# Values and ones in one tile, division by tokens, and PSUM drained by two engines in two attention layers

## The chip, the cores and the metric

The kernel runs on one core of a Trainium2 chip. Its engines are TensorE (PE in the profile; PEld are its weight loads), VectorE (DVE), ScalarE (ACT), GpSimd (POOL) and SyncE (SP, which issues most DMA transfers). The metric is the time of one execution on the device in microseconds; a version is told by the median of its runs.

## What is computed

The reference is a chain of eight layers, four attentions and four feed-forward layers, each applied to the layer-normed activation and added to it. The input is 8 batches of 512 tokens with 128 features. Only the first and the third layer matter here. Cut to their core:

```python
# first attention: 16 heads of 8
q, k, v = proj(Wq), proj(Wk), proj(Wv)
for start in range(0, S, 128):                 # queries start .. start+127
    scores = q[start:start+128] @ k[:start+128].T / sqrt(8)
    scores = where(triu(ones(128, start+128), k=1), neg, scores)
    out[start:start+128] = softmax(scores) @ v[:start+128]
y = out @ Wo

# second attention: linear, 64 features per head
qf, kf = relu(q @ Wf + bf), relu(k @ Wf + bf)
kv = einsum('blhf,blhd->bhfd', kf, v)
num = einsum('blhf,bhfd->blhd', qf, kv)
den = maximum(einsum('blhf,bhf->blh', qf, kf.sum(axis=1)), 1e-6)
y = (num / den) @ Wo + bo
```

The mask of the first attention hides, for the query with index i inside its window, every key with an index above i counted from the start of the sequence. So only the first 128 keys are ever seen, and one 128 x 128 triangle serves all four windows.

## The kernel before

The activation lives in SBUF as eight tiles `X[b]` of 128 tokens x 4 token blocks x 128 features. The function `l0_l1_ffn` runs the first four layers in one stage (the change is only there); later stages run the other four layers.

In that stage the work of a batch is a chain of generators, and each `yield` ends a piece. `scores` (first attention up to the maxima) and `exps` with `add_up` (exponentials and weighted sums, four head rows `r` per batch) and `give` (division, output projection) are followed by `experts` (the routed feed-forward layer), `features` (second attention) and `router` (router of the fourth layer). A loop at the end of the stage takes one piece of every generator in flight in each step, so that several batches overlap: in a step of even number the next `exps`, in a step of odd number the sums. A new batch starts every eight steps, and `scores` runs 13 steps ahead. After the last batch of the first attention, pieces of the shared experts (`shared`, L369 to L384) are put in between.

This is the program's order. A scheduler of the framework then fixes one order of instructions for each engine, which departs from it in places; each engine works through its own list in order and waits by semaphores where it needs another's result.

Heads are packed four to a 32-partition group. A group is called a quad here: four matmuls of 32 rows or 32 columns, one per quad, run side by side on the array.

- Scores, L533 to L551: for each token block `c`, four matmuls fill two PSUM tiles `halves` of two banks each (tag "two", two such tiles in all). ScalarE copies each half to `sm` (L542), GpSimd masks it (L543), VectorE reduces it to the negated maxima (L547).
- Exponentials, L558 to L581: scores again, keys on the partitions, plus the maxima by a second matmul, into the same two PSUM tiles; ScalarE takes the exponential into `eT` (L575, four buffers), GpSimd masks (L577).
- Sums, L584 to L594: for every row `r` one set of four matmuls with the values `vq` as the stationary operand into `o0`, and one set with `own`, a tile of ones, into `o1`: the latter holds the softmax sums, repeated 8 times over the partitions of a head. `vq` holds the values of head row `r` in the columns of that row and zeros elsewhere (L524).
- Division, L596 to L601: reciprocal of `o1`, 128 x 512, and a product with `o0`, both on VectorE. Then the output projection (L606).
- Second attention, L733 to L834: features of the keys (L762, L767 into "two", relu by ScalarE at L773 into `wide[:, 0]`), of the queries (L783, relu at L788 into `wide[:, 1]`), products `kv` with the values `v` and with a tile of ones `one` (L797), masking by head (L802), transposes (L262 through `flipped`), product with the query features for numerator and denominator (L814), then maximum, reciprocal, copy and product (L819 to L823) on VectorE, ScalarE and GpSimd.

PSUM has eight banks of 128 x 512 float32: four are the two tiles "two", two the tiles "mm" that everything else shares, and two `o0` and `o1`. The tile `wide` later takes the expert table of the fourth layer; its load is issued in the last batch of `features`. In the first ten steps after the leading ones, DMA transfers fill a DRAM buffer with zeros out of a tile `zeros`.

Of the kernel before, what the change touches and what calls it, by code (L numbers as in the profile page):

```python
# [67 lines left out]
def eight_layers(ctx: ExitStack, tc: tile.TileContext, w: dict, out: bass.AP):  # L68
# [171 lines left out]
    def cols(c):  # L240
        return slice(c * P, (c + 1) * P)
# [28 lines left out]
    def l0_l1_ffn():  # L270
# [28 lines left out]
        with ExitStack() as es:  # L299
# [101 lines left out]
            with ExitStack() as es1:  # L401
# [9 lines left out]
                own = keep.tile([P, 4, 4, HD], F32, tag="own", name="own")  # L411
                nc.gpsimd.memset(own, 1.0)
                nc.gpsimd.affine_select(
                    out=own, in_=own, compare_op=ALU.is_equal, fill=0.0, base=0,
                    pattern=[[1, 4], [-1, 4], [0, HD]], channel_multiplier=0,
                )
                own = own.rearrange("p r s d -> p r (s d)")
# [15 lines left out]

                maxima = [keep.tile([P, C, 4, 32], BF16, tag=f"mx{i}", name=f"mx{i}") for i in range(2)]
# [10 lines left out]
                zeros = keep.tile([P, C, 4, 32], F32, tag="zeros", name="zeros")  # L445
# [53 lines left out]
                one = keep.tile([P, 32], F32, tag="one", name="one")  # L499
                nc.vector.memset(one, 1.0)  # L500

                ready = {}

                def scores(b):

                    stats(b, mv0)
                    for got in normal(b, mv0, work):
# [15 lines left out]
                    vq = work.tile([P, 4, 4, 32], F32, tag="vq", name="vq", bufs=3)  # L523
                    nc.vector.tensor_tensor(  # L524
                        vq,
                        mm[:, P : 2 * P].rearrange("p (q f) -> p q f", q=4).unsqueeze(2)
                        .to_broadcast([P, 4, 4, 32]),
                        own.unsqueeze(1).to_broadcast([P, 4, 4, 32]), ALU.mult,
                    )
# [3 lines left out]
                    for c in range(C):  # L533
                        halves = [two("sc").rearrange("p i (r k) -> p (i r) k", k=P) for i in range(2)]
                        for q in range(4):
                            nc.tensor.matmul(  # L536
                                halves[q // 2][:, 4 * (q % 2) : 4 * (q % 2) + 4, :],
                                qT[quad(q), cols(c)], kb[quad(q)], start=True, stop=True,
                            )
                        for i in range(2):  # L540
                            sm = work.tile([P, 8, P], F32, tag="sm", name="sm", bufs=2)
                            nc.scalar.copy(sm, halves[i])  # L542
                            nc.gpsimd.affine_select(  # L543
                                out=sm, in_=sm, compare_op=ALU.is_ge, fill=-1e30, base=0,
                                pattern=[[0, 8], [-1, P]], channel_multiplier=1,
                            )
# [37 lines left out]
                def add_up(b, r, i, eT):  # L584

                    if r == 0:
                        sums_of[b, i] = ps.tile([P, S], F32, tag=f"o{i}", name=f"o{i}", bufs=1)
# [1397 lines left out]
```

## Time and profile before

| | |
|---|---|
| median of 3 runs | 1713.37 us (1712.08 to 1717.24) |
| profiled execution, its own time | 1725.08 us |
| its span from first to last instruction | 1723.3 us |
| PE busy | 1470.0 us, 85% of the span |
| PEld busy | 651.2 us, 38% |
| DVE busy | 1206.9 us, 70% |
| ACT busy | 796.6 us, 46% |
| POOL busy | 677.8 us, 39% |
| mean granted TensorE clock | 0.935 |
| first to last start of a first-attention exponential score matmul (L568) | 40.7 to 428.7 us |
| last start of a second-attention product (L814) | 607.6 us |

Busy times of one execution are added up by engine; matmuls overlap, so a busy PE need not be at its peak. A group of instructions is shown with its line, engine and operation, output and input tile, shapes and count, then busy us and mean ns of one, then the idle time of the engine just before them and whose work ended it. Lines are those of the kernel before.

### The profile page before, as it was taken

How to read it: one execution, taken by the hardware profiler on the slowest of the kernel's cores; microseconds unless marked ns; L12 is line 12 of the kernel's file. 1: busy time of each engine (PE TensorE's matmuls, PEld its weight loads, DVE VectorE, ACT ScalarE, POOL GpSimd, SP SyncE). 2: the span in 40 equal slices, each digit the busy share in tenths (PEclk: the TensorE clock that was granted, in tenths of full speed). 3: DMA queues.
4: the chain of work that ended last, by engine and by line, in shares of the span. 5: the costliest groups of instructions: out<-in, count | busy, mean ns of one | idle time of the engine just before them, and what ended most of it. 6: DMA issues, size and time to landing. Idle time of an engine off the chain costs nothing.

```text
span 1723.3 us, 22463 instructions
## 1 busy us (share of the span) xinstructions
PE 1470.0 (85%) x8060; PEld 651.2 (38%) x8061; DVE 1206.9 (70%) x2374; ACT 796.6 (46%) x1158; POOL 677.8 (39%) x728
## 2 busy tenths in 40 slices
PE   5978898899888868988999896977888888888887
PEld 2322333334344435644555453422222222233335
DVE  7688666655654444357775764589899999988765
ACT  3655655555454423353223230055555565565634
POOL 4754344443321140211213318135645645712750
PEclk8999899999899889988999898999899999999988
DMA  7991000000000022304544653634444444443201
GB/s 270 384 342 34 1 1 13 7 13 13 13 19 19 13 99 78 95 10 109 124 116 118 134 126 95 151 80 129 124 127 128 133 129 125 131 117 95 61 13 31
DMA packets 94224, 164.69 MB, mean 96 GB/s; under 512 B 10848, under 2 KB 36960, under 8 KB 90016
## 3 DMA queue, kind: packets, MB, share of 16 engines
q1 hardware_dynamic: 89392, 151.97, 31.4%
q0 software_dynamic: 3568, 9.18, 1.7%
q10 hardware_dynamic: 1152, 2.10, 0.4%
q8 instruction: 64, 1.05, 0.3%
q14 instruction: 48, 0.39, 0.1%
HBM read 110.27 MB, written 52.95 MB: 95 GB/s over the span
## 4 chain that ended last, share of the span: by engine, by line
PE 43%; DVE 28%; issue 10%; POOL 7%; ACT 5%; DMA 5%; SPq 1%; DVEq 0%; POOLq 0%; ACTq 0%
DVE h L1890 11%; PE key L1644 5%; PE acc L1622 5%; PE bx L1879 3%; DMA gx<-du_d 2%; PE mm L262 2%; PE sT L568 2%; DVE mf L547 2%; PE o L591 2%; PE sc L536 1%; PE gu L369 1%; PE gu L1055 1%; DMA gate<-gates 1%; DVE zx L1698 1%; PE Z L1690 1%
## 5 line engine op out<-in xcount | busy, mean ns | idle before, releaser
L1890 DVE TENSOR_TENSOR_SCAN h<-a,bx 128x1024 f32<-128x1024 f32 x192 | 426.9, 2269 | 29.2 <-PE bx L1879 27.7
L1885 ACT ACTIVATE a<-dr,nA 128x1022 f32<-128x1022 f32 x192 | 219.4, 1146 | 221.2 <-DVE h L1890 221.0
L1879 PE MATMUL bx<-gx,wb 64*128 64x512 f32 x768 | 220.2, 666 | 61.3 <-DVE h L1890 59.2
L1335 POOL TENSOR_TENSOR gx<-gx,xk 128x1024 f32<-128x1024 f32 x32 | 75.4, 2357 | 226.0 <-DMA gx<-du_d 194.3
L1644 PE MATMUL key<-xT,L_ffn_keys 128*128 128x512 f32 x256 | 136.4, 615 | 22.9 <-DVE act L1648 22.9
L1879 PEld LDWEIGHTS bx<-gx,wb 64*128 64x128 f32 x768 | 64.8, 195 | 195.1 <-DVE h L1890 149.8
L1622 PE MATMUL acc<-act,L_ffn_values 128*128 128x512 f32 x256 | 132.7, 602 | 0.0
L1648 DVE SCALAR_TENSOR_TENSOR act<-key,gate 128x512 f32<-128x512 f32 x128 | 86.5, 685 | 47.8 <-PE key L1644 34.6
L1690 PE MATMUL Z<-h,wc 64*32 64x512 f32 x1536 | 110.3, 628 | 0.1
L547 DVE TENSOR_REDUCE mf<-sm 128x8 f32<-128x1024 f32 x64 | 76.1, 1211 | 42.5 <-POOL sm L543 42.4
L577 POOL TENSOR_SCALAR_AFFINE_SELECT eT<-eT 128x1024 f32<-128x1024 f32 x64 | 68.9, 1099 | 78.7 <-ACT eT L575 78.7
L543 POOL TENSOR_SCALAR_AFFINE_SELECT sm<-sm 128x1024 f32<-128x1024 f32 x64 | 69.4, 1098 | 71.2 <-ACT sm L542 70.9
L1433 POOL DMA_INDIRECT back<-f_out,back_at x32 | 30.8, 964 | 155.7 <-DVE bn L248 139.3
L542 ACT COPY sm<-sc 128x1024 f32<-128x1024 f32 x64 | 62.5, 1014 | 54.7 <-PE sc L536 40.6
L1410 ACT COPY oT<-acc 128x512 f32<-128x512 f32 x8 | 4.7, 587 | 159.2 <-PE acc L1622 159.2
L575 ACT ACTIVATE eT<-sT 128x1024 f32<-128x1024 f32 x64 | 62.0, 1021 | 28.0 <-PE sT L568 27.9
L1644 PEld LDWEIGHTS key<-xT,L_ffn_keys 128*128 128x128 f32 x256 | 47.1, 195 | 73.2 <-issue 36.2
L1622 PEld LDWEIGHTS acc<-act,L_ffn_values 128*128 128x128 f32 x256 | 49.1, 193 | 60.0 <-issue 60.0
L536 PE MATMUL sc<-kb,qT 32*128 32x512 f32 x256 | 58.9, 724 | 10.0 <-ACT sm L542 4.1
L248 DVE BATCH_NORM_STATS2 bn<-x 128x6 f32<-128x128 f32 x224 | 56.1, 272 | 4.8 <-DMA x<-in_L_attn_hidden_states 4.0
L1116 POOL TENSOR_TENSOR rstd<-rstd,minus_half 128x4 f32<-128x4 f32 x27 | 28.0, 1040 | 80.0 <-DVE rstd L1115 79.8
L568 PE MATMUL sT<-qT,kb 32*128 32x512 f32 x256 | 55.2, 655 | 4.5 <-ACT sm L542 2.9
(482 smaller groups left out, 3006.4 us busy)
## 6 DMA issues: line engine op xcount, KB each, us to landing
f_in<-zeros SPq DMA_DIRECT2D x10, 3584.0 KB
gate<-gates SPq DMA_DIRECT2D x128, 256.0 KB
dr<-dt_d SPq DMA_DIRECT2D x32, 1024.0 KB
gx<-du_d SPq DMA_DIRECT2D x128, 128.0 KB
xk<-xh_d SPq DMA_DIRECT2D x32, 256.0 KB
wide<-in_L_ffn_experts SPq DMA_DIRECT2D x1, 3072.0 KB
xg<-f_in SPq DMA_DIRECT2D x48, 64.0 KB
f_out<-ys SPq DMA_DIRECT2D x12, 256.0 KB
```

The costliest lines, as they stand in the source:

```text
L536: nc.tensor.matmul(halves[q // 2][:, 4 * (q % 2) : 4 * (q % 2) + 4, :], qT[quad(q), cols(c)], kb[quad(q)], start=True, stop=True,)
L543: nc.gpsimd.affine_select(out=sm, in_=sm, compare_op=ALU.is_ge, fill=-1e30, base=0, pattern=[[0, 8], [-1, P]], channel_multiplier=1,)
L547: nc.vector.tensor_reduce(mf[:, c, 2 * i : 2 * i + 2], sm.rearrange("p (q r) k -> p q r k", q=2), AX.X, ALU.max, negate=True,)
L568: nc.tensor.matmul(halves[q // 2][:, q % 2, :], lhs[quad(q), r, :], rhs[quad(q)], start=(k == 0), stop=(k == 1),)
L1335: nc.gpsimd.tensor_tensor(gx, gx, xk.unsqueeze(1).to_broadcast([P, 2, S]), ALU.mult)
L1622: nc.tensor.matmul(acc, f2_v[:, j, :], act, start=(j == 0), stop=(j == J - 1))
L1644: nc.tensor.matmul(key, f2_k[:, 2 * j : 2 * j + 2, :], xT, start=True, stop=True)
L1648: nc.vector.scalar_tensor_tensor(act, key, 0.0, gate[:, j % 2, :], ALU.max, ALU.mult)
L1690: nc.tensor.matmul(zs[q][32 * j : 32 * j + 32, i, :], wcf[half, g, :], hs[j // 2][half, j % 2, :], start=(g == 0), stop=(g == G - 1),)
L1879: nc.tensor.matmul(bx[:, k, :], wbf[half, g, :], gx[half, j, :], start=True, stop=True,)
L1885: nc.scalar.activation(a[:, :, 1:], dr[:, 2 * j : 2 * j + 2, 1:], AF.Exp, scale=nA[:, q, g : g + 1],)
L1890: nc.vector.tensor_tensor_scan(h.rearrange("p r t -> p (r t)"), a.rearrange("p r t -> p (r t)"), bx.rearrange("p r t -> p (r t)"), 0.0, AL ...
```

## The change

For the first attention, the values and a block of ones now share one stationary tile: of its 32 columns, for two heads 8 columns of values and 8 of ones each. Three such tiles are kept and their zeros and ones are written once by GpSimd; per batch VectorE copies in only the values (four copies). One set of matmuls per row gives values and sums together; rows 0 and 1 go to `o0`, rows 2 and 3 to `o1`. For the second attention the tile `vo` does the same, with `kv`, its mask (`m2` in place of `m4`), its transposes and the final product in half the matmuls.

The division is a new generator, `divided`, used by both attentions: ScalarE copies the two PSUM tiles to `both`; TensorE transposes them, so that tokens are on the partitions and a head's sum is one number; VectorE takes reciprocals of 32 numbers per token block set and multiplies; the result `a` is transposed back (`flipped`, with ScalarE's copy to `aT`).

In the scores, the second half is masked by a bfloat16 matmul that adds `later_keys` (0 or -1e30) through the identity, and VectorE reduces it straight out of PSUM; the first half goes the old way. The relus of the second halves of key and query features move from ScalarE to VectorE. `eT` has two buffers in place of four, `zeros` is a part of `wide`, and `own` and `one` are gone.

```diff
+                def divided(tiles, least):
+                    both = work.tile([P, 2, S], F32, tag="both", name="both", bufs=2)
+                    for i in range(2):
+                        nc.scalar.copy(both[:, i], tiles[i])
+                    yield True
+                    a = work.tile([P, C, D], F32, tag="toks", name="toks", bufs=2)
+                    for i in range(2):
+                        mm = mm_four()
+                        for c in range(C):
+                            nc.tensor.transpose(mm[:, c, :], both[:, i, cols(c)], ident)
+                        mm = mm.rearrange("p c (n k d) -> p (c n) k d", k=2, d=HD)
+                        rd = work.tile([P, 8 * C, 1], F32, tag="rd", name="rd", bufs=2)
+                        if least is None:
+                            nc.vector.reciprocal(rd, mm[:, :, 1, 0:1])
+                        else:
+                            nc.vector.tensor_scalar(rd, mm[:, :, 1, 0:1], least, None, ALU.max)
+                            nc.vector.reciprocal(rd, rd)
+                        nc.vector.tensor_tensor(
...
+                    yield True
+                    aT = work.tile([P, S], F32, tag="aT", name="aT", bufs=2)
+                    flipped(a, mm_four(), aT)
+                    yield aT
...
-                zeros = keep.tile([P, C, 4, 32], F32, tag="zeros", name="zeros")
+                zeros = wide[:, 0, 0]
...
+                    vq = values[b % 3]
+                    v4 = mm[:, P : 2 * P].rearrange("p (q r d) -> p q r d", q=4, r=4)
+                    for r in range(4):
+                        nc.vector.tensor_copy(vq[:, :, r, r % 2, 0, :], v4[:, :, r, :])
...
-                        for i in range(2):
-                            sm = work.tile([P, 8, P], F32, tag="sm", name="sm", bufs=2)
-                            nc.scalar.copy(sm, halves[i])
-                            nc.gpsimd.affine_select(
...
+                        for q in range(2, 4):
+                            nc.tensor.matmul(
+                                halves[1][:, 4 * q - 8 : 4 * q - 4, :], identb, later_keys,
+                                start=False, stop=True,
+                            )
+                        sm = work.tile([P, 8, P], F32, tag="sm", name="sm", bufs=2)
+                        nc.scalar.copy(sm, halves[0])
+                        nc.gpsimd.affine_select(
...
+                        for i, x in ((1, halves[1]), (0, sm)):
                             nc.vector.tensor_reduce(
                                 mf[:, c, 2 * i : 2 * i + 2],
...
                         nc.tensor.matmul(
-                            o[quad(q)], vq[:, q, r, :] if i == 0 else own[:, r, :],
-                            eT[q // 2][:, q % 2, :], start=(r == 0), stop=(r == 3),
+                            o[quad(q)], vq[:, q, r, :], eT[q // 2][:, q % 2, :],
+                            start=(r % 2 == 0), stop=(r % 2 == 1),
                         )
...
-                    nc.vector.reciprocal(rd, sums_of.pop((b, 1)))
-                    aT = work.tile([P, S], F32, tag="aT", name="aT", bufs=2)
-                    nc.vector.tensor_tensor(aT, rd, sums_of.pop((b, 0)), ALU.mult)
-                    yield True
-                    yield True
+                    for got in divided([sums_of.pop((b, i)) for i in range(2)], None):
+                        yield True
+                    aT = got
...
+                        nc.scalar.activation(here[:, 0:2], halves[0], AF.Relu)
+                        nc.vector.tensor_scalar(here[:, 2:4], halves[1], 0.0, None, ALU.max)
...
+                        nc.scalar.activation(qf[:, 0:2, i, :], halves[0], AF.Relu, bias=a1_bf2)
+                        nc.vector.tensor_scalar(
+                            qf[:, 2:4, i, :], halves[1], a1_bf2, 0.0, ALU.add, ALU.max
+                        )
...
-                    for k in (1, 0):
-                        for i in range(2):
-                            for q in range(4):
-                                nc.tensor.matmul(
-                                    o[quad(q), k, :], kt[:, 2 * k + i, quad(q)], qf[:, q, i, :],
-                                    start=(i == 0), stop=(i == 1),
-                                )
...
+                    for i in range(2):
+                        for q in range(4):
+                            nc.tensor.matmul(
+                                o[quad(q), i, :], kt[:, i, quad(q)], qf[:, q, i, :],
+                                start=True, stop=True,
+                            )
+                    for got in divided((o[:, 0], o[:, 1]), 1e-6):
+                        yield True
```

In the loop, the sums of a row now follow in the odd step as one set, where before the set of values came one step later; `give` starts in the odd step too.

## The prediction

> **What bounds the kernel now.** I first cut the span into stretches, because the change touches only the first stage (two attentions, the expert layer between them, the router). The columns are the length, then busy us and instruction count for PE, PEld, DVE, ACT and POOL, then the granted TensorE clock, the DMA share and GB/s.
>
> ```profile
> 40.00:430.00 390.00, 337.64 (x2182) 131.69 (x2183) 263.76 (x636) 222.27 (x273) 183.35 (x194) 0.94 0.26 92
> 430.00:620.00 190.00, 159.95 (x1045) 77.36 (x1046) 95.93 (x294) 87.35 (x121) 47.74 (x55) 0.91 0.10 34
> ```
>
> From 40 to 430 us all eight first attentions run, with expert layers and second attentions of earlier batches between them; from 430 to 620 us only the latter and shared-expert matmuls are left. PE is busy 87% and 84%, so it idles 52 + 30 = 82 us; no other engine passes 68%. All the rest of the span (620 to 1723 us) does the same work after the change.
>
> Second, the groups by line, for what the change touches, and third, PE's waits in the two stretches:
>
> ```profile
> L547 DVE TENSOR_REDUCE mf<-sm 128x8 f32<-128x1024 f32 x64 | 76.1, 1211 | 42.5 <-POOL sm L543 42.4
> L542 ACT COPY sm<-sc 128x1024 f32<-128x1024 f32 x64 | 62.5, 1014 | 54.7 <-PE sc L536 40.6 <-DVE mf L547 13.7
> L591 PE MATMUL o<-eT,own 128*32 128x512 f32 x256 | 44.4, 605 | 0.4 <-POOL eT L577 0.4
> L788 ACT ACTIVATE wide<-qq,a_bf 128x1024 f32<-128x1024 f32 x32 | 34.2, 1111 | 21.4 <-PE qq L783 21.2 <-ACT xT L265 0.2
> L599 DVE RECIPROCAL rd<-o 128x512 f32<-128x512 f32 x8 | 26.8, 3348 | 1.6 <-PE o L591 1.6
> L822 DVE RECIPROCAL rd<-rd 128x512 f32<-128x512 f32 x8 | 26.8, 3346 | 0.0
> ```
> ```profile
> PE mm L751 <- DVE x L831: 13.3, 3, 5.2
> PE mm L606 <- DVE aT L601: 7.8, 2, 7.0
> PEld sT L568 <- ACT sm L542: 20.9, 23, 2.0
> PEld sc L536 <- ACT eT L575: 10.9, 15, 1.1
> PE mm L830 <- POOL aT L823: 8.4, 4, 5.5
> ```
>
> A reciprocal of 128x512 costs 3.35 us, and PE twice waited (7.8 us) for the division at L601 behind it and four times (8.4 us) for the one at L823. The chain that ended last, cut to 0 to 650 us, holds six reciprocals of each line (3.27 us apiece, 39 us), 28 us of the reduce L547 and 14 us of the mask L543. So PE is nearly full, and what breaks it up is VectorE's long instructions and the draining of the two-bank PSUM tiles ("two", two of them), which ScalarE does alone.
>
> **The change part by part, on PE.** Durations are merged stretches of the timeline between 240 and 282 us, where four quadrant matmuls run side by side (a float32 matmul is recorded as two):
>
> ```profile
> 241.18 3.62 PE L814 MATMUL o<-wide,kt 128*32 128x512 f32 x32
> 244.73 0.66 PE L262 MATMUL mm<-ident,xn 128*128 128x128 f32 x4
> 274.11 1.06 PE L591 MATMUL o<-eT,own 128*32 128x512 f32 x8
> 277.46 1.16 PE L606 MATMUL mm<-L_attn_Wo,aT 128*128 128x128 f32 x8
> 278.56 0.39 PE L713 MATMUL mm<-wT,sel 32*128 32x512 bf16 x1
> ```
>
> - Values and ones in one stationary tile: the sums with "own" go, 8 batches x 4 rows x 1.06 = -34 us.
> - Second attention, L814: half of 32 records, 8 x 3.62/2 = -14.5.
> - L797 (3.45 us a batch in the chain): as many instructions, 128 columns instead of 256. Between half (1.7) and nothing saved; I take 1.2, since its weight loads stay (16 us of PEld busy in all, 2 a batch): 8 x 1.2 = -9.
> - Two of four transposes of km: 8 x 0.2 = -2.
> - Division by tokens: 12 transposes per batch and attention, 192. Bounds: 192 x 0.11 (0.44 us of a 0.66 us group of four is spacing) = 21, and 48 groups x 0.66 = 32; eight adjacent at 1.1 and four at 0.66, sixteen times, make +28.
> - The mask of the second half as a matmul: 64 full-array bf16 matmuls of 512 columns. The nearest row, L721 (same shape and type), has a median of 389 ns, alone: 64 x 0.389 = 25. The Trainium skill ("TensorE: Matmul & The Clock Gate", What happens when you issue a matmul) gives 216 ns from start to start when they follow each other: 64 x 0.216 = 14. Against the change speaks "TensorEngine Tiling (Array Packing)", Key Properties: switching between 32-row tiles and the full array drains the engine, and each of the 32 pairs is such a switch, there and back. The last two rows above are one: L606, full array, ends at 278.62, and L713, 32 rows, has started at 278.56; no gap is seen (matmul ends are modelled). By the row the pair follows at once, by the rule it costs its own latency. I take 18, between the two, and keep 14 and 25.
>
> Sum on PE: -59.5 + 28 + 18 = -13.5 us (bounds about -25 and 0).
>
> **On the other engines.** VectorE loses L599 and L822 (53.6), L819 and L601 (10.9), the values' multiply L524 (5.4), 2.1 of L802: -72. It gains 32 relus of 128x1024 out of PSUM (L819 has 0.688 us for 512, so 1.22): 39; 32 small copies of values at 0.17: 5; 32 reciprocals of 32 elements (between 0.17 us for 4 and 3.35 for 512: 0.34): 11; 16 maxima at 0.19: 3; 32 products of 256 (0.68 for 512, so 0.42): 13. Together +71: nothing in sum, but its longest piece falls from 3.35 to 1.22 us. Its 32 reduces of "sc" instead of "sm" read PSUM; by L819 against L547 that costs no more than 0.02 each. ScalarE: -31 (half of L542), -33 (half of L773 and L788), -4.7 (L821), -2 (kt), +19 (32 copies of 512 at 0.59), +9.4 (16 copies of aT): -42. GpSimd: -35 (half of L543), -10 (L823), about +4.5 of setup memsets: -41. None is the fullest engine, so these count only through waits:
>
> - Waits for the long divisions: L606 on L601 7.8, L830 on L823 8.4, and L713 on L607 7.8 (two), which sits behind the same queue. The copies to "both" release the sums in 2 x 0.59, and transposes, division and flip come one loop step apart, each step being some 6 us, with other work between. I take two thirds of 24: -16. If that cover is gone, PE stands in front of the flipped tile instead and this gain is 0.
> - "two" halves drained by two engines: PE's waits on sm, eT and wide (L773, L788) come to some 60 us of weight-load idle, but most of it lies under running matmuls (the PE rows for the same are under 20 us in all). Of the first halves nothing changes; the second come free about 1 us sooner. -8 (bounds -25 and +10).
> - New: 48 more "mm" tiles, 32 of which only VectorE releases. PE's three waits for L831 (13.3 us) show what a late VectorE costs. One in sixteen at 4.4 us: +8 (bounds 0 and +30).
> - Start: GpSimd's order has now the wait for f_g (landed at 11.99) and the third batch's statistics (13.17) ahead of the first rstd power, which ran at 7.95; the first xn moves from 10.84 to about 14.5: +3.7. The first scores lose one ScalarE copy and one mask per column block, where ScalarE had waited for L547 time after time up to 35 us: -5. Net -1.
> - The second attention has one more loop step (after its last batch too): about a step of the tail, (620-430)/46 = 4 us, partly filled by shared experts: +3. The table load into "wide" moves two steps back; it ends near 620 us and is first used at 671.7, so 50 us hide it; without them 8 us would show. The zero fill now reads "wide", but the last such DMA starts at 91.4 and the first feature is written at 201.5. Halving eT's buffers costs nothing: PE runs add_up of one row ahead of the next row's sT anyway.
>
> Sum: -13.5 - 16 - 8 + 8 - 1 + 3 = -27.5 us. The profiled execution took 1725.1 us (span 1723.3), so its like would be 1697.6; the median of the runs, 1713.4, becomes 1686.
>
> **The rivals.**
> - *VectorE late as a drain (slower).* It now releases 64 "two" halves and 32 "mm" tiles, in order, in a queue that also waits: L547 waited 42.4 us for the mask, and second-attention relus stand behind the router's chain of small instructions. Each drain caught behind it stops PE, as with L831 at 4.4 us. The gain of 27.5 is eaten when six more are caught (0.3 us per drain on average); with fifteen, +66 - 27.5 = +38: 1752; just past the point 1720 to 1730. For it: VectorE stays at 68%. Against: no instruction over 1.8 us is left in it there, and it waits less for GpSimd.
> - *PE alone counts.* Waits only change names: -13.5 + 3, so about 1703; with the dear mask and transposes (-59.5 + 32 + 25 = -2.5) no change, 1711 to 1716. For it: 87% busy.
> - *The chain through VectorE and GpSimd was the real limit.* The 39 us of reciprocals and half of the 42 us of L547 and L543 go, short divisions of 1.5 us (12 x 1.5 = 18) come: -42, and PE's -13.5: 1658. For it: this chain holds the stage up to 200 us. Against: PE has only 82 us of idle time.
>
> **How the numbers follow.** Forecast (1668 to 1705, PE alone at its middle included) 0.54; limit in VectorE and GpSimd, below 1668, 0.16; no gain left, 1705 to 1719, 0.12; VectorE late, above 1719, 0.18. A measurement of this kernel tells 0.3% (5 us: 1708.2 to 1718.5) from no change. That band gets half of the third case, 0.07; faster 0.74; slower 0.19, the last case and a little of the third. The range goes from the third rival with PE's -25 for its -13.5, 1646, to 1724, in the middle of the slower one's 1720 to 1730.
>
> **What would show it.** Right: L591 with 256 records and some 45 us; the page's reciprocal rows gone from the costly groups; the stretch to the last second attention about 27 us shorter with PE still above 85% busy; transposes of "both" near 0.11 to 0.17 us each of busy; the last matmuls of "later_keys" at 0.2 to 0.4 each. Wrong: PE waits on "wide", "mf" or "toks" of VectorE of over 30 us in all; DVE above 75% there; or a stretch after 620 us that differs.

## The result: slower, 1770.6 us against 1715.3

Runs of both kernels give a median of 1770.64 us after (1763.50 to 1782.88, four runs) and 1715.30 us before (1712.08 to 1718.50, four runs). The ratio is 1.033, its 95% interval 1.026 to 1.040. The forecast was 1686 us with a range from 1646 to 1724: wrong in direction, and the time lies outside the range. Of all executions below, one (of values_fill, 1752.84 us) fell in a slower state of the chip and is left out of that run's figures.

The profiled execution took 1763.5 us (span 1761.7); that of before took 1725.1 (1723.3). Three marks in the two timelines say where the time went. The last two exponentials of the first attentions start at 429.6 us before and at 483.4 after: +53.8. From there to the end of the last product of the second attention it is 178.6 us before and 172.4 after. The first scan of a later layer starts at 1129.8 and at 1179.2: +49.4. So the loss arises while the eight first attentions run. The part from that scan to the end, which is the same program in both, took 593.6 us before and 582.6 after; over all traces of this document it lies between 582.6 and 594.3, so single executions differ by up to 12 us there. Here are the two stretches of the prediction after the change (length, then busy us and count of PE, PEld, DVE, ACT, POOL, then granted clock, DMA share, GB/s):

```profile
40.00:430.00 390.00, 327.60 (x1710) 136.21 (x1730) 205.92 (x587) 169.82 (x217) 129.49 (x141) 0.82 0.26 90
430.00:620.00 190.00, 163.57 (x1123) 81.92 (x1118) 108.63 (x383) 90.17 (x134) 51.46 (x63) 0.95 0.04 15
```

In the first stretch every engine is less busy than before (VectorE 206 us for 264, ScalarE 170 for 222, GpSimd 129 for 183): the same 390 us now get less work done. No engine became the bound by its busy time. And TensorE's granted clock fell from 0.94 to 0.82.

To compare equal work, here is the stretch from 40 us to the last two exponentials, first before, then after:

```profile
40.00:429.58 389.58, 337.22 (x2178) 131.27 (x2179) 263.76 (x636) 221.85 (x273) 183.35 (x194) 0.94 0.26 92
```
```profile
40.00:483.36 443.36, 376.40 (x2048) 158.74 (x2067) 236.35 (x701) 197.95 (x257) 149.30 (x164) 0.84 0.23 81
```

Of the 53.8 us more, PE was busy for 39.2 and idle for 14.6. So the smaller part of the loss stands in the trace as waiting, the larger as longer busy time at a lower clock. Busy time multiplied by the clock is an estimate of the matmul work at full clock: 317 us before, 316 after. It is rough, since it gives 303 and 322 in sc_first and relu_old (below), which have the same matmuls as the change.

The groups that answer to those shown of before (0 to 700 us; line, operation, out<-in, count, busy us, mean ns of one, then the idle time before them and its releaser):

```profile
L637 PE MATMUL o<-eT,vq 128*32 128x512 f32 x256 | 44.1, 655 | 0.4 <-POOL eT L622 0.4
L591 DVE TENSOR_REDUCE mf<-sm 128x8 f32<-128x1024 f32 x32 | 38.9, 1215 | 68.5 <-POOL sm L586 68.5
L591 DVE TENSOR_REDUCE mf<-sc 128x8 f32<-128x1024 f32 x32 | 38.9, 1214 | 3.4 <-PE sc L580 3.4
...
L436 PE MATMUL mm<-ident,both 128*128 128x128 f32 x128 | 21.5, 312 | 0.0
...
L580 PE MATMUL sc<-later_keys,identb 128*128 128x512 bf16 x44 | 19.7, 501 | 4.0 <-issue 4.0
L818 DVE TENSOR_SCALAR wide<-kq 128x1024 f32<-128x1024 f32 x16 | 19.5, 1217 | 8.0 <-PE kq L812 7.9
```

The reads out of PSUM cost what was expected (1.214 us for the reduce, 1.217 for the relu), and L637 has its 256 records and 44 us. The odd row is the second: half as many reduces of `sm` as before, yet they wait longer for GpSimd, 68.5 us instead of 42.4. The waits show the rest (engine, line, what it waited for: us in total, times, longest; 40 to 650 us):

```profile
DVE mf L591 <- POOL sm L586: 65.5, 16, 7.6
PEld sT L613 <- DVE mf L591: 47.6, 19, 5.0
PE sT L613 <- DVE mf L591: 33.8, 16, 4.7
...
PE qq L825 <- DVE wide L818: 7.9, 2, 5.1
...
PE sc L575 <- DVE wide L830: 7.3, 3, 2.5
```

For 33.8 us PE could not write the exponentials' scores, because a reduce (`mf`, L591) had not freed the PSUM tile; before, it waited 3.7 us in all there (2.9 for the copy to `sm`, 0.8 for a relu). The weight loads ahead of these matmuls show the same wait, and the last two rows are the new relus of VectorE as late drains. With the smaller rows PE waited 40 us for `mf` and 19 us for VectorE's relus: the prediction's own sign of being wrong, over 30 us. The chain that ended last goes through this wait again and again. From 108 to 117 us (start, us, what):

```profile
108.18 2.03 PE sc L575 x6
...
110.24 1.02 ACT sm L585
...
111.32 1.10 POOL sm L586
...
112.44 2.36 DVE mf L591 x2
...
114.85 1.17 PE sT L613 x2
```

And the timeline says what the two reduces in the fourth of these pieces are (start, us, engine, line, what, then idle time before it):

```profile
110.41 0.75 PE L580 MATMUL sc<-later_keys,identb 128*128 128x512 bf16 x2
...
112.44 1.22 DVE L591 TENSOR_REDUCE mf<-sm 128x8 f32<-128x1024 f32 x1 [7.24 <-POOL sm L586]
...
113.58 1.21 DVE L591 TENSOR_REDUCE mf<-sc 128x8 f32<-128x1024 f32 x1
...
114.85 0.70 PE L613 MATMUL sT<-qT,kb 32*128 32x512 f32 x2 [0.55 <-DVE mf L591]
```

The half that is masked by matmul is ready at 111.16. VectorE is idle then: it has waited 7.24 us for the other half, the one that goes by ScalarE and GpSimd. Only after that one is reduced does it read the ready half, and only then is the PSUM tile free. The program writes the reduce out of PSUM first (`for i, x in ((1, halves[1]), (0, sm))`); the scheduler put the reduce of `sm` ahead of it, in 31 of the 32 blocks. The half that should have come free "about 1 us sooner" comes free later than before: behind the copy, the mask and both reduces.

### The profile page after: what moved, and what is told of

The parts are those of the page before. It is cut to its first block, busy times and chain, and to the rows that moved or that the text cites. A ratio compares the mean times of both kernels' runs of the same rounds, so it can differ in the third digit from the quotient of the medians.

```text
span 1761.7 us, 22144 instructions
## 1 busy us (share of the span) xinstructions
PE 1500.1 (85%) x7896; PEld 677.6 (38%) x7917; DVE 1179.7 (67%) x2478; ACT 757.0 (43%) x1134; POOL 634.4 (36%) x704
## 4 chain that ended last, share of the span: by engine, by line
PE 45%; DVE 26%; issue 10%; POOL 8%; DMA 5%; ACT 4%; SPq 1%; DVEq 0%; POOLq 0%; ACTq 0%
DVE h L1927 11%; PE key L1681 4%; PE acc L1659 4%; PE sT L613 3%; PE bx L1916 3%; DVE mf L591 3%; PE sc L575 2%; DMA f_in<-xr,to 2%; PE mm L262 2%; DMA gate<-gates 2%; PE mm L1287 2%; PE Z L1727 2%; PE gu L369 1%; PE gu L1092 1%; DVE zx L1735 1%
## 5 line engine op out<-in xcount | busy, mean ns | idle before, releaser
L622 POOL TENSOR_SCALAR_AFFINE_SELECT eT<-eT 128x1024 f32<-128x1024 f32 x64 | 68.5, 1091 | 187.5 <-ACT eT L620 187.5
L613 PE MATMUL sT<-qT,kb 32*128 32x512 f32 x256 | 76.6, 732 | 35.7 <-DVE mf L591 33.8
L575 PE MATMUL sc<-kb,qT 32*128 32x512 f32 x256 | 73.5, 835 | 16.5 <-DVE wide L830 7.3
L1470 POOL DMA_INDIRECT back<-f_out,back_at x32 | 30.7, 961 | 155.5 <-DVE bn L248 139.0
L591 DVE TENSOR_REDUCE mf<-sm 128x8 f32<-128x1024 f32 x32 | 38.9, 1215 | 68.5 <-POOL sm L586 68.5
L917 POOL DMA_INDIRECT f_in<-xr,to x32 | 32.5, 1014 | 89.1 <-DVE to L913 49.1
L586 POOL TENSOR_SCALAR_AFFINE_SELECT sm<-sm 128x1024 f32<-128x1024 f32 x32 | 35.0, 1093 | 58.8 <-ACT sm L585 58.7
```

Of the source, the lines that this page charges most:

```text
L575: nc.tensor.matmul(halves[q // 2][:, 4 * (q % 2) : 4 * (q % 2) + 4, :], qT[quad(q), cols(c)], kb[quad(q)], start=True, stop=(q < 2),)
L591: nc.vector.tensor_reduce(mf[:, c, 2 * i : 2 * i + 2], x.rearrange("p (q r) k -> p q r k", q=2), AX.X, ALU.max, negate=True,)
L613: nc.tensor.matmul(halves[q // 2][:, q % 2, :], lhs[quad(q), r, :], rhs[quad(q)], start=(k == 0), stop=(k == 1),)
L622: nc.gpsimd.affine_select(out=e4, in_=e4, compare_op=ALU.is_ge, fill=0.0, base=0, pattern=[[0, 8], [1, P]], channel_multiplier=-1,)
```

## The experiments

Times are medians, with the ratio to the kernel before, run beside it, and its 95% interval. The median of before lies between 1715 and 1720 us in these series. A profiled execution can lie 12 us off its kernel's median (relu_old), so ends are compared by medians and traces are used for places.

### Which part is dear

The first four runs take the changed kernel apart. First, an edge (a dependency added by hand) that fixes the order of the two reduces:

```diff
+                        done = []
                         for i, x in ((1, halves[1]), (0, sm)):
-                            nc.vector.tensor_reduce(
+                            done.append(nc.vector.tensor_reduce(
...
+                        tc.add_manual_dep(
+                            done[1].ins, done[0].ins.name,
+                            mybir.DependencyInfo(mybir.DependencyClass.NoSync, mybir.DependencyReason.DATA),
+                            reason="order",
+                        )
```

> The changed kernel with one ordering edge between the two reduces of a score block: on VectorE the reduce that reads PSUM (sc) stands ahead of the one that reads the masked copy (sm) in all 32 blocks, where the changed kernel has it behind in 31 of 32. Theory A (VectorE's order holds the second PSUM tile until ScalarE's copy, GpSimd's mask and the other reduce are done, and TensorE idles and is clocked down): the 34 us of TensorE waits of sT on mf fall below 12, the clock from 40 to 430 us rises from 0.82 to over 0.90, the time falls by 50 to 85 us, to 1685 to 1720. Theory B (the mask matmuls and switches between 32-row tiles and the full array cost TensorE time themselves): less than 20 us gained, 1750 or more. Theory C (VectorE is overloaded by the relus and small products): less than 20 us gained, 1750 or more.

Measured: 1741.41 us, 1.0114 (1.004 to 1.019), so 29 us faster than the change: more than theories B and C allowed, less than A asked for. The wait in question and the first stretch, in its trace, and the mask matmuls, for all 64 of which it has records:

```profile
PE sT L619 <- DVE mf L592: 22.5, 9, 4.4
```
```profile
40.00:430.00 390.00, 340.34 (x1900) 144.83 (x1898) 223.34 (x663) 187.77 (x245) 139.24 (x152) 0.83 0.26 91
```
```profile
L580 PE MATMUL sc<-later_keys,identb 128*128 128x512 bf16 x64 | 24.9, 480 | 0.0
```

The wait fell by a third, not below 12 us, and the clock stayed at 0.83 where theory A expected over 0.90. So the 29 us came back without a higher clock. The edge turns the two reduces round in the 31 blocks, and the scheduler moves some more with it (by the traces 26 further places of VectorE's 2478), so the 29 us are the price of that order with what it drags along.

Second, the change with the scores of before (copy, mask and reduce of `sm` for both halves, no mask by matmul):

```diff
-                        for q in range(2, 4):
-                            nc.tensor.matmul(
-                                halves[1][:, 4 * q - 8 : 4 * q - 4, :], identb, later_keys,
...
-                        sm = work.tile([P, 8, P], F32, tag="sm", name="sm", bufs=2)
-                        nc.scalar.copy(sm, halves[0])
...
+                        for i in range(2):
+                            sm = work.tile([P, 8, P], F32, tag="sm", name="sm", bufs=2)
+                            nc.scalar.copy(sm, halves[i])
```

> The changed kernel with the scores as before: both halves copied by ScalarE, masked by GpSimd, reduced out of sm; no mask matmuls. Theory A and theory B both: the loss goes, 1680 to 1720, clock back above 0.90; theory A says it does no better than the run with sc ahead of sm by more than 20 us, theory B says it does better by 30 us or more. Theory C (relus on VectorE): stays above 1745.

1743.05 us, 1.0151 (1.008 to 1.023): the same as sc_first within the intervals, which are some 13 us to either side. In the order written, no gain or loss by the new scores shows here; in the scheduler's order they cost 28 us.

Third, the change with all relus on ScalarE:

```diff
-                        nc.vector.tensor_scalar(here[:, 2:4], halves[1], 0.0, None, ALU.max)
+                        nc.scalar.activation(here[:, 2:4], halves[1], AF.Relu)
...
-                        nc.vector.tensor_scalar(
-                            qf[:, 2:4, i, :], halves[1], a1_bf2, 0.0, ALU.add, ALU.max
-                        )
+                        nc.scalar.activation(qf[:, 2:4, i, :], halves[1], AF.Relu, bias=a1_bf2)
```

> The changed kernel with all relus of the features on ScalarE again. Theory C: falls to 1720 or less. Theory A: the waits on wide of L818 and L830 (19 us on TensorE) go and ScalarE waits take part of their place; 0 to 15 us gained, 1755 to 1770.

1765.21 us, 1.0255 (1.020 to 1.031): about 5 us less than the change by medians, 13 by the ratios, and within the intervals, while the late reduces are still there.

Fourth, six more matmuls of 512 columns ahead of each exponential's scores, into a PSUM tile that is then overwritten. They raise the load on PE and change no result:

```diff
+                    for n in range(6):
+                        nc.tensor.matmul(
+                            halves[0][:, n % 2, :], to_all[:, r, :], later_keys.rearrange("p r k -> p (r k)"), start=True, stop=True,
+                        )
                     for k, (lhs, rhs) in enumerate(((kb, qT), (to_all, mxT))):
```

> The changed kernel with six bf16 matmuls of 512 columns (about 1.3 us) put into the first sT tile ahead of the real ones, which overwrite them; VectorE's order is left as it is, so the wait for the second tile stays. It tells how much of the loss is the clock of TensorE alone. Theory A with the clock as amplifier: clock from 40 to 430 us rises from 0.82 to 0.90 or more, matmuls shorten, time falls by 10 to 35 us in spite of 32 x 1.3 = 42 us of added matmul time, most of it in gaps. Without the clock as a cause (waits alone): no gain, between 0 and +40 us, 1770 to 1810.

1774.34 us, 1.0321 (1.026 to 1.038), with the clock at 0.86 in the first stretch instead of 0.82. The 192 matmuls are 50 us of busy time in its trace (1.6 us for six; the 1.3 of the expectation are six times the 0.216 us quoted in the prediction), and the time is that of the change within the intervals, as was expected for waits alone. Still, this does not clear the clock. The filler is work itself: up to the last exponentials PE was busy 400.3 us at 0.87, an estimated 348 us at full clock, where the change has 316. What the higher clock gave may have gone into it.

### Each part alone

Values, ones and division by tokens alone, which is the change with two of the edits just shown, of the scores and of the relus:

> The changed kernel with scores and relus both as before: left are values and ones in one tile and the division by tokens. On TensorE this part takes away 59.5 us and adds 28 by the prediction's terms. If TensorE's time were the limit: 1675 to 1695. If the limit is the chain from engine to engine, and TensorE with less to do is clocked down instead (0.85 in the run with the old scores against 0.94 before): no faster than before, 1715 to 1745, with TensorE's clock from 40 to 430 us at 0.88 or less.

1723.92 us, 1.0035 (1.001 to 1.006): about 6 us slower, where my sum had a large gain. The relus of the second halves alone, in the kernel before (the relu edit the other way round):

> The kernel before with only the relus of the second halves moved to VectorE (39 us of work), which here keeps both long reciprocals. Draining by two engines as predicted: 0 to 10 us faster. VectorE as a late drain: 5 to 25 us slower.

1738.74 us, 1.0113 (1.009 to 1.014): 20 us slower. Its PE waits from 40 to 650 us:

```profile
PE kq L762 <- DVE wide L773: 10.7, 4, 5.2
...
PE sc L536 <- DVE wide L773: 4.2, 2, 3.8
PE sc L536 <- DVE wide L785: 3.7, 3, 1.3
```

With two smaller rows (0.7 and 0.5), PE waited 19.8 us for VectorE's relus, and its waits for those of ScalarE went only from 11.5 us before to 10.2. That is the size of the 20 us lost. The relu itself takes 0.2 us more on VectorE (1.22 and 1.28 us for 1.02 and 1.12 on ScalarE), some 6 us for 32; what is late is its turn in VectorE's list. One block of key features shows it:

```profile
342.68 1.02 ACT L772 ACTIVATE wide<-kq 128x1024 f32<-128x1024 f32 x1 [1.54 <-PE kq L767]
343.58 0.18 DVE L690 RECIPROCAL w<-w 128x4 f32<-128x4 f32 x1 [4.05 <-POOL w L688]
...
347.36 1.22 DVE L773 TENSOR_SCALAR wide<-kq 128x1024 f32<-128x1024 f32 x1
...
348.63 0.70 PE L536 MATMUL sc<-kb,qT 32*128 32x512 f32 x2 [3.75 <-DVE wide L773]
```

ScalarE starts its half as soon as the matmuls are done. VectorE, whose half is ready then too, first waits for GpSimd with a small reciprocal and then works through other small instructions of its list; it starts 4.7 us later, and PE waits 3.75 us for it.

The new scores alone, in the kernel before (the change's lines for them, with the edge of the first experiment):

> The kernel before with only the scores changed (second half masked by a matmul and reduced out of PSUM), the PSUM reduce ahead of the other on VectorE. If draining by two engines shortens the wait for PSUM as predicted: 8 to 25 us faster although it adds 64 mask matmuls. If the mask matmuls cost 14 to 25 us of TensorE that counts: 0 to 20 us slower.

1724.52 us, 1.0048 (1.002 to 1.008): 6 us slower. Even in the order written the reduce out of PSUM is a late drain. PE waited for `mf` before the exponentials' scores for 22.9 us here, and for 19.7 us in sc_first_relu_old (below), where PE had waited 3.7 us in all before. One such place:

```profile
152.97 3.35 DVE L618 RECIPROCAL rd<-o 128x512 f32<-128x512 f32 x1
...
155.12 0.38 PE L548 MATMUL sc<-later_keys,identb 128*128 128x512 bf16 x1 [0.16 <-issue]
...
159.85 0.23 DVE L690 TENSOR_TENSOR rc<-rc,ln_r 128x64 f32<-128x64 f32 x1 [2.04 <-POOL ln_r L688]
159.99 1.22 DVE L560 TENSOR_REDUCE mf<-sc 128x8 f32<-128x1024 f32 x1
...
161.26 1.22 PE L587 MATMUL sT<-qT,kb 32*128 32x512 f32 x2 [4.02 <-DVE mf L560]
```

The half is ready at 155.5 and is read at 160.0, behind the long reciprocal and a chain of small instructions that waits for GpSimd.

### What a microsecond of matmuls is worth

The kernel before without the ones sums of head rows 1 to 3, so the division uses the sums of row 0 only; 24 sets go, 25 us at the 1.06 us of a set from the prediction:

```diff
+                        if i == 1 and r > 0:
+                            continue
                         nc.tensor.matmul(
-                            o[quad(q)], vq[:, q, r, :] if i == 0 else own[:, r, :],
-                            eT[q // 2][:, q % 2, :], start=(r == 0), stop=(r == 3),
+                            o[quad(q)], vq[:, q, r, :] if i == 0 else every[:, 0:32],
+                            eT[q // 2][:, q % 2, :], start=(r == 0), stop=(r == 3 or i == 1),
```

> The kernel before with three of four matmul sets on the ones tile left out (rows 1 to 3; the softmax sums are then those of row 0 of each group only, so the output differs), nothing put in their place and all else left: 24 fewer sets per three quarters of the rows, 24 x 1.06 = 25 us of TensorE. It prices a microsecond of TensorE in this stage. If TensorE is the limit: 20 to 27 us faster, 1692 to 1700. If the chain through the other engines is: 0 to 8 us faster, and the clock from 40 to 430 us falls from 0.94 to 0.90 or less.

1730.02 us, 1.0070 (1.005 to 1.009): work taken away from the fullest engine, and 12 us slower. Two things came with it: the clock fell, and the scheduler's lists shifted (by the traces 93 of VectorE's 2374 instructions stand elsewhere). To tell these apart, the same kernel with the 25 us put back as three more copies of row 0's values set, overwritten by the real one, which leaves ScalarE's list as it is and moves only four instructions of VectorE's and one of GpSimd's:

```diff
+                    if i == 0 and r == 0:
+                        for n in range(3):
+                            for q in range(4):
+                                nc.tensor.matmul(
+                                    o[quad(q)], vq[:, q, r, :], eT[q // 2][:, q % 2, :],
+                                    start=True, stop=True,
+                                )
```

> ones_gone (1730 us; the sets of sums of rows 1 to 3 left out, so the division uses the sums of row 0 alone) with the values' set of row 0 given three more times, 24 sets of about 1.06 us in all, so that TensorE has its 25 us of matmuls back while every other engine keeps the order of ones_gone. If less matmul work was itself the harm, through the granted clock (0.88 in the 40 to 430 us of ones_gone, 0.94 before): clock back to 0.92 or more and 1715 to 1721 us. If the order that moved with the removal was the harm: 1729 us or more, and up to 1755 if the work costs its full price on top.

1730.26 us, 1.0065 (1.003 to 1.010): equal to ones_gone. So by medians putting the work back costs nothing, and with that its removal was worth nothing; the 12 us came along with the edit otherwise. The shifted lists (all 93 places lie between 67 and 451 us) are the likeliest cause, but it is not shown: the other values that the edit makes also reach every later layer, and the traces do not show the loss. In them (one execution of each, and those of the two runs are 6 to 7 us below their medians) the last product of the second attention ends at 608.2 us before, at 607.2 without the work and at 617.8 with it. The first stretch, without the work, then with it back:

```profile
40.00:430.00 390.00, 325.66 (x1941) 128.89 (x1943) 261.57 (x628) 221.31 (x271) 182.75 (x194) 0.88 0.27 92
```
```profile
40.00:430.00 390.00, 332.86 (x2051) 130.71 (x2048) 254.18 (x612) 214.97 (x263) 178.73 (x189) 0.90 0.27 92
```

The clock follows the work a little, 0.88 to 0.90. My expectation asked for 0.92 and a shorter time if the clock were the cause. The clock did not get there, and the time did not move.

The same from the other side: values_only with the sum sets of even rows given three times (32 sets more, 34 us, and the lists of VectorE, ScalarE and GpSimd are the same):

```diff
-                    for q in range(4):
+                    for n in range(3 if r % 2 == 0 else 1):
+                        for q in range(4):
...
-                            start=(r % 2 == 0), stop=(r % 2 == 1),
+                                start=(r % 2 == 0), stop=(r % 2 == 1 or n < 2),
```

> The run values_only (scores and relus as before) with the sums' matmul set of every even row done three times, each overwriting the last: 32 sets more, as many as the ones tile had, 32 x 1.06 = 34 us of TensorE that the output does not need; every other engine's order is the same. If TensorE's time is the limit: 25 to 34 us slower than values_only, about 1750. If TensorE with less work is only clocked down: between 12 us faster and 8 us slower than values_only (1712 to 1732), with the clock from 40 to 430 us back from 0.85 to 0.90 or more.

1725.73 us (five runs), 1.0045 (1.001 to 1.008): about 2 us for 34. Where the rest went is seen by laying three traces beside each other in the first stretch. The kernel before, exponentials' scores and scores (mean ns of one matmul after the busy us):

```profile
L568 PE MATMUL sT<-qT,kb 32*128 32x512 f32 x256 | 55.2, 655 | 4.5 <-ACT sm L542 2.9 <-ACT wide L788 0.8
L536 PE MATMUL sc<-kb,qT 32*128 32x512 f32 x216 | 46.7, 698 | 4.1 <-ACT wide L788 3.6 <-DVE kb L519 0.2 <-ACT eT L575 0.2
```

The same two groups in values_only, with its row of the stretch:

```profile
L575 PE MATMUL sc<-kb,qT 32*128 32x512 f32 x224 | 58.6, 807 | 16.8 <-ACT eT L614 9.1 <-DVE kb L560 5.6 <-ACT wide L811 1.0
L607 PE MATMUL sT<-qT,kb 32*128 32x512 f32 x246 | 58.5, 703 | 3.2 <-ACT sm L581 2.3 <-ACT wide L823 0.8
```
```profile
40.00:430.00 390.00, 336.60 (x1897) 142.06 (x1889) 222.47 (x666) 232.30 (x293) 175.21 (x186) 0.85 0.26 91
```

And in values_fill:

```profile
L575 PE MATMUL sc<-kb,qT 32*128 32x512 f32 x224 | 57.7, 777 | 14.8 <-ACT eT L614 7.3 <-DVE kb L560 5.5 <-ACT wide L824 0.9
L607 PE MATMUL sT<-qT,kb 32*128 32x512 f32 x240 | 49.1, 660 | 4.9 <-ACT sm L581 4.1 <-ACT wide L824 0.6
```
```profile
40.00:430.00 390.00, 343.76 (x2121) 141.22 (x2113) 223.27 (x662) 230.16 (x291) 174.25 (x186) 0.89 0.26 91
```

The change of the values left PE as busy as before, 336.6 us for 337.6. The new transposes fill a part of what was taken out, and the matmuls that stayed got longer: the exponentials' scores went from 655 to 703 ns, the scores from 698 to 807, while the clock went from 0.94 to 0.85. Putting 34 us in brought the clock to 0.89 and the exponentials' scores back to 660 ns; PE's busy time rose by 7 us only (by 11 up to the last exponentials). What is counted as busy is in part a slower clock.

### Both dear parts taken out

The change with the edge of sc_first and the relus on ScalarE, and the same with the fill of values_fill:

> The changed kernel without its two dear pieces: the PSUM reduce ahead of the other, and all relus on ScalarE. If the loss is these two (29 us from the order, about 19 from the relus): 1717 to 1730. If they overlap, so that one still costs what both did: 1735 to 1745.

> The run sc_first_relu_old with the same 34 us of repeated sums. If the clock answers to TensorE's work: within 10 us of the run without, clock from 40 to 430 us higher by 0.03 or more; if TensorE's time counts: 20 to 34 us slower.

The first took 1720.24 us, 1.0005 (0.997 to 1.004): level with the kernel before, and 50 us faster than the change. The second took 1741.28 us, 1.0108 (1.007 to 1.015). Here 34 us of matmuls cost 18 to 21 us, many times what they cost in values_fill, and the clock rose only from 0.86 to 0.87. Up to the last exponentials PE's busy time rose by 24 us (354.6 to 378.3). The lists of the other engines are the same in both. Why the clock doesn't rise here is not settled.

### The start

The first exponential starts at 43.2 us before, at 47.9 after and at 50.5 in sc_first_relu_old. Two attempts to win that back in the latter: the scaling `gs`, which waits for a load of f_g, moved from the setup into the first `experts`; then also the ones of `vo` moved into the first `features`, and edges that keep each batch's first rstd power (`y`) ahead of the next batch's statistics (`x`) on GpSimd.

```diff
-                nc.gpsimd.tensor_scalar(gs, f0_g, 1.0 / E, None, ALU.mult)
...
+                    if b == 0:
+                        nc.gpsimd.tensor_scalar(gs, f0_g, 1.0 / E, None, ALU.mult)
```

> The run sc_first_relu_old with GpSimd's scaling of the router's gain, which waits for a transfer, moved from the setup into the first expert layer, so that it no longer stands ahead of the first rstd. The third batch's statistics still do. If the late start reaches the end: 2 to 5 us faster than sc_first_relu_old; if the third batch's statistics are what counts: no difference, first exponential within 1 us.

```diff
-                nc.gpsimd.memset(vo, 1.0)
...
+                    if b == 0:
+                        nc.gpsimd.memset(vo, 1.0)
...
+                if mv is mv0:
+                    if b:
+                        tc.add_manual_dep(
+                            x.ins, rooted[b - 1].ins.name,
...
+                    rooted[b] = y
```

> The changed kernel with the reduce out of PSUM first and the relus on ScalarE (1720 us, level with before), and on GpSimd the first rstd power of each batch ahead of the next batch's statistics, the scaling gs and the ones of vo later. If the late start (first exponential at 50.5 us against 43.2 before) is passed on to the end: first exponential at 44 to 47 us and 1713 to 1717 us, faster than before by a little. If the lateness is taken up by waits further on, as when gs alone was moved: 1718 to 1723 us.

They took 1722.26 us, 1.0013 (0.998 to 1.004), and 1720.86 us, 1.0017 (0.998 to 1.005). The first exponential came at 48.1 and 48.5 us, so only 2 of the 7 us were won, and nothing of them shows at the end. The second missed the 44 to 47 us that it was made for, so what a start as early as before is worth stays open.

No version here is faster than the kernel before.

## Why the prediction was wrong

By medians, the parts add up as follows. The kernel before is put at 1718; values and division bring 1724 (+6); the relus on VectorE 1743 (+19); the new scores in the order written 1741 (-2); the scheduler's order of the two reduces 1770 (+29). The parts are not independent: the relus cost 19 to 21 us in three settings but 5 while the reduces are late, and the order costs 29 us with the new relus and 45 with the old (1720 to 1765).

So two sums failed. Scores and relus were put at +10 (the mask +18, the drains -8) and came to +47. Values, division, loop and start were put at -37.5 and came to +6. The first made the change slow; the second took its gain. The prediction's steps, one by one:

- **"The second come free about 1 us sooner. -8 (bounds -25 and +10)": the step that made it slow.** It took the order of the program for the order of the engine. In VectorE's list the late operand stands first, and a ready tile waits behind it. For the reduces, with the mask's work in it, the new scores come to between -4 (sc_first_relu_old against values_only) and +6 (scores_alone) in the order written. In the scheduler's order they come to +28, and to +41 with the relus on ScalarE (relu_old against values_only). That list could be read before the run; I looked for what left VectorE, not for what stood in front of the new reduce. (The waits on ScalarE's drains that the term starts from were 76 us on the weight loads and 22 on PE, for my 60 and 20.)
- **Relus "nothing in sum".** The durations were right (1.22 predicted, 1.217 and 1.282 measured) and VectorE is far from full, but they are drains now, each behind whatever VectorE has queued. This is the rival "VectorE late as a drain", whose deciding point was six more waits of 4.4 us, some 26 us. In relu_alone 19.8 us of such waits went with 20 us of time. The rival was right in mechanism; I gave it too small a chance and counted no place for it in the sum. The Trainium skill ("TensorEngine Tiling (Array Packing)", PSUM Bottleneck) advises using both ScalarE and VectorE for evacuation. Here giving VectorE a half was worse than ScalarE alone, by 20 us.
- **"PE sum -13.5".** The terms were fair in size where the clock allows a comparison: L637 came to 44 us as foreseen. The transposes were dear: 33 us of busy time (21.5 for L436 and 11.9 for the flipped ones) for a forecast of 28. So was the mask by matmul. The change's own trace has only 44 of its 64 records, but sc_first has all of them: 24.9 us, the dearer of the two bounds; I took 18. That is the row of before (0.389 us each) and not the 0.216 us that the Trainium skill states ("TensorE: Matmul & The Clock Gate", What happens when you issue a matmul). Its rule on switching tile sizes ("TensorEngine Tiling (Array Packing)", Key Properties) does not show: no gap stands in front of those 64, and the 20 gaps (4.0 us) in front of L580 in the change's trace all stand where one record of a pair is missing. But the error is that the sum was booked as time. By medians PE's 25 us were worth 0 in ones_refill, 34 us were worth 2 in values_fill and 50 were worth 4 in fill_wait; only in sc_first_relu_old_fill did 34 us cost 18 to 21. "PE nearly full" was read from a busy share that holds when the clock falls.
- **"Waits for the long divisions -16".** As waits most of them went: of 24 us of PE's waits for L601, L823 and L607, 2.6 are left (L650, the former L607), and 5.5 us for L442 and L444 came. In values_only some 13 us came. As time they did not come back: values_only, which has all of that, is 6 us slower. What holds its first stretch instead isn't settled; among the largest waits of PE there, 40 to 650 us, are 9.1 us of scores for the exponentials (L614) and 9.1 us of transposes for VectorE's `xr`, which was 0.2 before. The two buffers of `eT` are in it too and were not tried alone; in its trace no exponential is seen to wait for the sums that free one.
- **New "mm" tiles +8:** in size right as waits, the 5.5 us just named; what they cost in time was not tried alone.
- **Start "net -1":** +4.7 us, since the first normalised activation came at 14.30, as said, but the scores did not win 5 us back. The 2 us that late_gs won there do not show at the end.
- **One more loop step +3:** not seen. From the last exponentials to the last product it is 6 us less than before.

What stays open is how much of the loss goes through PE's waits and how much through its clock. sc_first shows that the order costs 29 us at an unchanged clock; of the 53.8 us in the trace of the change, 39.2 stand as longer busy time.

## What to carry to other kernels

Where a scheduler fixes each engine's list, look in that list for what stands in front of every instruction that frees a buffer; a freeing instruction behind one with a late operand undoes the gain, and one added edge may mend it (29 us here). Moving a drain to another engine is paid by where it stands in that engine's list more than by its duration: here 32 relus that are 0.2 us longer cost 20 us. Before booking saved matmul time as gain, put some in: if a filler costs nothing in that very build, don't book the saving. The answer holds for that build only: the same 34 us cost 2 us in one and 18 to 21 in another.

## What was not expected of the hardware

The clock that TensorE is granted went with the matmul work put in or taken out. It was 0.94 in the first stretch of the kernel before, 0.88 with 25 us of matmuls left out and 0.90 with as much put back; 0.85 with the values' change and 0.89 with 34 us added; 0.82 in the change and 0.86 with 50 us added. The Trainium skill ("TensorE: Matmul & The Clock Gate", What's actually happening) has the gate set by how busy TensorE has been lately, and the direction agrees in all of these. But the busy share that the profile counts does not tell the clock: PE was busy for 87% of the first stretch both before and in sc_first, at 0.94 and at 0.83. Busy time multiplied by the clock, up to the last exponentials, roughly follows the work (estimates: 317 us before, 291 in ones_gone, 313 in ones_refill; 300 in values_only, 320 in values_fill), while busy time alone moved by 17 us for the 25 put back and by 11 for the 34. So in these traces a part of a saving went into a lower clock. One pair (0.86 to 0.87, with 18 to 21 us lost) shows that added work is not always paid back by a higher one. I had read the clock as given, and all durations as fixed.
